# An order from 600 drawn-up plans in place of one list schedule, in a fused two-layer block with conditioning

## The chip, the cores and the metric

One core of one Trainium2 chip. The metric is device time in microseconds (us) of one execution; lower is better. One more execution was taken with the hardware profiler, and all rows below come from it.

## The reference

Two sequences of 2048 rows with 512 features each, and one vector of 512 per sequence that conditions them:

```python
emb = jnp.dot(jax.nn.silu(t), ada_w) + ada_b
shift_msa, scale_msa, gate_msa, shift_mlp, scale_mlp, gate_mlp = jnp.split(emb, 6, axis=-1)
norm = _ln(x) * (1.0 + scale_msa[:, None]) + shift_msa[:, None]
h = jax.nn.gelu(jnp.dot(norm, ssm_w1) + ssm_b1, approximate=False)
x = x + gate_msa[:, None] * (jnp.dot(h, ssm_w2) + ssm_b2)
norm2 = _ln(x) * (1.0 + scale_mlp[:, None]) + shift_mlp[:, None]
hf = jax.nn.gelu(jnp.dot(norm2, ff_w1) + ff_b1, approximate=True)
return x + gate_mlp[:, None] * (jnp.dot(hf, ff_w2) + ff_b2)
```

The weights ssm_w1 and ssm_w2 are 512x512, ff_w1 is 512x1024, ff_w2 1024x512, ada_w 512x3072; all is float32.

## The kernel before, in words

The 4096 rows are cut into eight blocks of 512. A block passes norm1, the first product (`ssm1`), the second product (`ssm2`), and norm2; after all eight, pairs of blocks (`s` = 0 to 3) pass the wide product (`ff1`) and then, block by block, the last one (`ff2`). All products are done with fewer multiplications and more additions: operands are split into quarters, seven products P1 to P7 replace eight, and in the ff stages this is done twice over. The additions on operands and results run on VectorE (DVE) and GpSimd (POOL), copies and activations on ScalarE (ACT), transfers are issued by SyncE (SP) and, a few, by ScalarE. Each float32 matmul of the program shows in the trace as two passes of TensorE (PE).

Nothing is issued while the program is described. `plan.add` records an `Op`: the engines that may do it (`"vg"` is VectorE or GpSimd), its cost and latency in ns on each, its size if it is a transfer, and its dependencies, found from the cells of the tiles that it reads and writes. `tt` (L256 in the profile) records a tensor-tensor op, `mm` (L294) a matmul, `turn` (L591) a transpose of VectorE, `stats` (L522 and L523) the mean and variance of a row, `act` (L274) and `copy` (L283) work of ScalarE, `dma` (L316) a transfer. So one line of the profile stands for many places, and the tiles' names (`bank` is PSUM, `hidden`, `ring`, `turned`, `near`, `far`, `rows`, `fw` are regions of SBUF that several stages share) tell them apart.

`Plan.order` then draws up the order. TensorE's order is that of the description and never changes. Every TensorE op is given a due time as if TensorE never waited; going backwards, every other op gets `late`, the latest time at which it may start for its successors' sake. `simulate` runs all engines forward by the recorded costs: whenever an engine is free, of the ops that could start first it takes the one with the earliest `late` (with a few rules about ops that become ready shortly, about transfers and about the SBUF port that VectorE and GpSimd share, `lock`). The whole is done twice, the second time with the due times moved by the wait found at the anchor, the first matmul of the first block's `ssm1`. The order of the starts is the order in which the ops are issued to the engines; on the chip each engine runs its own queue in this order and waits by semaphores.

The diff touches `Plan` alone; all stages call it through `plan.add`, and it is called at the end:

```python
for op in plan.order():
    op.done = op.fn(plan.engines[op.on])
    if op.after:
        tc.add_manual_dep(op.done.ins, op.after.done.ins.name, behind, reason="port")
```

Of the kernel before, what the change touches and what calls it, by code (L numbers as in the profile page):

```python
# [1 line left out]

# [12 lines left out]


class Op:
    __slots__ = ("n", "engs", "fn", "cost", "lat", "shared", "size", "lead", "care", "after", "done", "sooner", "deps", "succ", "late", "on", "start", "end", "note")


class Plan:
# [11 lines left out]
    LITTLE = 1 << 15  # L33
    LANES = 8
    AHEAD, SLACK = 2500.0, 150.0

    def __init__(self, nc):
        self.nc = nc
        self.engines = {"p": nc.tensor, "v": nc.vector, "a": nc.scalar, "g": nc.gpsimd, "s": nc.sync}
        self.ops, self.wrote, self.read, self.known = [], {}, {}, {}  # L40
        self.stage, self.care = "", 0.0
# [44 lines left out]
        return op  # L86

    def order(self):
        ops = self.ops
        for op in ops:  # L90
            if op.engs == "p":
                op.deps = {d for d in op.deps if ops[d].engs != "p"}
            for d in op.deps:
                ops[d].succ.append(op.n)
        t, due = 0.0, {}
        for op in ops:
            if op.engs == "p":
                due[op.n] = t
                t += op.cost["p"]
        for _ in range(2):  # L100
            for op in reversed(ops):
                late = due.get(op.n, 1e9)
                for s in op.succ:
                    late = min(late, ops[s].late - (1 + op.care) * (self.HOP + min(op.lat.values()) + op.size / self.RATE))
                op.late = late - op.sooner
            self.simulate()
            wait = ops[self.anchor].start - due[self.anchor]
            due = {n: t + wait for n, t in due.items()}
        return sorted(ops, key=lambda op: (op.start, op.n))

    def simulate(self):
        ops, hop = self.ops, self.HOP
# [1386 lines left out]
```

## Time and profile before

| | |
|---|---|
| median of 3 runs | 566.54 us (566.49 to 567.19) |
| the profiled execution's own time | 566.59 us |
| its span, first to last instruction | 564.8 us |
| granted TensorE clock | 1.000 |
| busy: TensorE, VectorE, GpSimd, ScalarE | 557.8, 483.1, 379.0, 266.0 us |
| DMA | 119.85 MB, mean 212 GB/s |

A timeline row reads: start, duration, engine, line, operation, tiles out<-in, partitions x elements, how many, and in brackets the engine's idle time before it and what ended it. Equal neighbours are merged into one row. A group's row gives busy time and the mean length of one record, then the idle time before its records. A row of waits gives total, count and longest. Of a matmul the end is modelled, and records of neighbours overlap.

### The profile page before, as it was taken

How to read it: one execution, taken by the hardware profiler on the slowest of the kernel's cores; microseconds unless marked ns; L12 is line 12 of the kernel's file. 1: busy time of each engine (PE TensorE's matmuls, PEld its weight loads, DVE VectorE, ACT ScalarE, POOL GpSimd, SP SyncE). 2: the span in 40 equal slices, each digit the busy share in tenths (PEclk: the TensorE clock that was granted, in tenths of full speed). 3: DMA queues.
4: the chain of work that ended last, by engine and by line, in shares of the span. 5: the costliest groups of instructions: out<-in, count | busy, mean ns of one | idle time of the engine just before them, and what ended most of it. 6: DMA issues, size and time to landing. Idle time of an engine off the chain costs nothing.

```text
span 564.8 us, 10322 instructions
## 1 busy us (share of the span) xinstructions
PE 557.8 (99%) x3553; PEld 506.3 (90%) x3553; DVE 483.1 (86%) x918; ACT 266.0 (47%) x534; POOL 379.0 (67%) x514
## 2 busy tenths in 40 slices
PE   8999999999999999999999999999999999999997
PEld 4888889888898988889999889999889999888997
DVE  5696978888879989898989899999999888789776
ACT  3473856674888845557102347212366122336120
POOL 2887638979826687995547866776776784446660
PEclk9999999999999999999999999999999999999999
DMA  8953799989799879895047899078956041820022
GB/s 315 398 221 87 233 343 308 316 240 320 223 268 369 257 271 273 273 323 185 4 147 255 302 286 332 18 204 282 321 172 198 2 151 46 272 95 28 1 75 74
DMA packets 53057, 119.85 MB, mean 212 GB/s; under 512 B 5473, under 2 KB 10509, under 8 KB 51470
## 3 DMA queue, kind: packets, MB, share of 16 engines
q1 hardware_dynamic: 51842, 118.66, 63.9%
q8 instruction: 28, 0.46, 0.3%
q10 hardware_dynamic: 1164, 0.55, 0.3%
q14 instruction: 23, 0.19, 0.1%
HBM read 77.63 MB, written 40.51 MB: 209 GB/s over the span
## 4 chain that ended last, share of the span: by engine, by line
PE 94%; DVE 3%; DMA 1%; issue 1%; POOL 0%; SPq 0%; DVEq 0%
PE bank L294 94%; DMA fw<-in_L_cond_ada_w_dram 1%; DVE hidden L256 1%; DVE near L256 0%; DVE marks L522 0%; PE bank L304 0%; POOL hidden L256 0%; POOL near L256 0%; SPq L316 0%; DVE rows L256 0%; DVE ring L256 0%; DVE fw L256 0%; DVE far L591 0%; DVE turned L656 0%; DVE marks L523 0%
## 5 line engine op out<-in xcount | busy, mean ns | idle before, releaser
L294 PE MATMUL bank<-turned,ring 128*128 128x256 f32 x896 | 208.7, 380 | 0.2 <-DVE turned L656 0.2
L294 PEld LDWEIGHTS bank<-turned,ring 128*128 128x128 f32 x896 | 167.6, 190 | 22.9 <-DVE turned L656 0.5
L256 DVE TENSOR_TENSOR hidden<-bank,hidden 128x512 f32<-128x512 f32 (+1 forms) x171 | 125.2, 755 | 28.0 <-PE bank L294 24.8
L294 PE MATMUL bank<-near,hidden 128*128 128x256 f32 (+1 forms) x470 | 95.3, 350 | 0.3 <-DVE rows L256 0.2
L294 PEld LDWEIGHTS bank<-near,hidden 128*128 128x128 f32 x470 | 82.1, 190 | 10.0 <-DVE rows L256 0.6
L294 PE MATMUL bank<-fw,hidden 128*128 128x128 f32 x640 | 90.4, 275 | 0.0
L256 DVE TENSOR_TENSOR rows<-bank,rows 128x128 f32<-128x128 f32 (+3 forms) x154 | 78.8, 554 | 11.4 <-PE bank L294 10.9
L294 PE MATMUL bank<-ring 128*128 128x256 f32 x336 | 82.4, 381 | 0.5 <-DVE hidden L256 0.5
L294 PEld LDWEIGHTS bank<-fw,hidden 128*128 128x128 f32 x640 | 81.2, 192 | 0.4
L283 ACT COPY bank<-bank 128x512 f32<-128x512 f32 (+2 forms) x88 | 37.3, 425 | 83.3 <-PE bank L294 82.2
L256 POOL TENSOR_TENSOR turned<-turned 128x512 f32<-128x512 f32 (+1 forms) x56 | 63.1, 1139 | 16.7 <-ACT turned L274 9.4
L294 PEld LDWEIGHTS bank<-ring 128*128 128x128 f32 x336 | 63.2, 190 | 11.2 <-issue 1.7
L294 PE MATMUL bank<-fw,far 128*128 128x128 f32 (+2 forms) x644 | 67.6, 278 | 0.7 <-DMA fw<-in_L_cond_ada_w_dram 0.7
L294 PEld LDWEIGHTS bank<-fw,far 128*128 128x128 f32 (+1 forms) x644 | 60.9, 167 | 2.7 <-issue 1.7
L274 ACT ACTIVATE hidden<-hidden,cols 128x512 f32<-128x512 f32 (+1 forms) x66 | 45.0, 712 | 37.9 <-DVE hidden L256 37.8
L294 PE MATMUL bank<-fw,near 128*128 128x128 f32 (+1 forms) x452 | 61.1, 279 | 0.0
L256 POOL TENSOR_TENSOR hidden<-hidden 128x128 f32<-128x128 f32 (+2 forms) x52 | 43.6, 847 | 22.6 <-DVE hidden L256 6.4
L294 PEld LDWEIGHTS bank<-fw,near 128*128 128x128 f32 x452 | 56.0, 192 | 0.4
L256 POOL TENSOR_TENSOR fw<-fw 128x256 f32<-128x256 f32 (+1 forms) x52 | 45.0, 875 | 13.3 <-DVE fw L256 7.7
L274 ACT ACTIVATE turned<-turned,mod,mod 128x512 f32<-128x512 f32 x56 | 41.5, 805 | 8.2 <-DMA turned<-turned 7.2
L256 POOL TENSOR_TENSOR ring<-turned,ring 128x256 f32<-128x256 f32 x37 | 27.8, 757 | 15.8 <-PE bank L294 9.7
L256 DVE TENSOR_TENSOR hidden<-hidden 128x512 f32<-128x512 f32 (+2 forms) x58 | 34.9, 621 | 1.2 <-ACT hidden L274 0.8
(136 smaller groups left out, 692.4 us busy)
## 6 DMA issues: line engine op xcount, KB each, us to landing
ring<-fw_parts SPq DMA_DIRECT2D x28, 512.0 KB
turned<-far SPq DMA_DIRECT2D x52, 256.0 KB
ring<-fw_parts SPq DMA_DIRECT2D x28, 384.0 KB
rows<-x SPq DMA_DIRECT2D x32, 256.0 KB
turned<-turned SPq DMA_DIRECT2D x32, 256.0 KB
out_dram<-rows SPq DMA_DIRECT2D x28, 256.0 KB
fw_parts<-fw SPq DMA_DIRECT2D x21, 256.0 KB
fw<-in_L_cond_ada_w_dram SPq DMA_DIRECT2D x5, 1024.0 KB
```

Of the source, the lines that this page charges most:

```text
L256: lambda E: E.tensor_tensor(o, a, b, f),
L274: lambda E: E.activation(o, a, func, bias=bias, scale=scale),
L283: plan.add("a", lambda E: E.copy(o, a), [o], [a], {"a": cost}, {"a": cost + 60})
L294: lambda E: E.matmul(o, lhsT, rhs, start=start, stop=stop, skip_group_check=True, **kw),
```

## The change

`order` first draws up the same plan as before (`draw_up` with an empty `wanted`, twice, with the same shift of the due times in between). Then it makes 600 rounds. In each it changes `wanted`, a table of ops that are to be placed some time sooner (their `late` is lowered): it picks one wait of TensorE behind the anchor, longer waits more often, goes from the inputs that were late there back by up to eight steps along the latest inputs, and wants the op found there sooner by a multiple of the wait; in 3 of 10 rounds it also drops one older wish. The plan is drawn up anew by the unchanged `simulate`, and `follow` then runs its sequence, with the order on every engine fixed, in three cases: transfers that land 700 ns after their data has passed, 2200 ns, and 1200 ns at 85% of the rate. The cost of a plan is the mean of TensorE's end over the three. A worse plan may be kept on the way, by up to 300 ns at first and less and less later; the best one found is issued. The random numbers have a fixed seed. The ops, their costs, their dependencies and TensorE's order are the same; `simulate` is not changed.

```diff
+    ROUNDS, WARMTH, LEAST = 600, 300.0, 30.0
+    CASES = ((700.0, 1.0), (2200.0, 1.0), (1200.0, 0.85))
...
     def order(self):
...
-        t, due = 0.0, {}
-        for op in ops:
-            if op.engs == "p":
-                due[op.n] = t
-                t += op.cost["p"]
-        for _ in range(2):
-            for op in reversed(ops):
-                late = due.get(op.n, 1e9)
-                for s in op.succ:
-                    late = min(late, ops[s].late - (1 + op.care) * (self.HOP + min(op.lat.values()) + op.size / self.RATE))
-                op.late = late - op.sooner
-            self.simulate()
-            wait = ops[self.anchor].start - due[self.anchor]
-            due = {n: t + wait for n, t in due.items()}
-        return sorted(ops, key=lambda op: (op.start, op.n))
+        tensor = [op for op in ops if op.engs == "p"]
+        t = 0.0
+        for op in tensor:
+            op.due, t = t, t + op.cost["p"]
+        self.draw_up({})
+        wait = ops[self.anchor].start - ops[self.anchor].due
+        for op in tensor:
+            op.due += wait
+        draw = random.Random(1)
+        wanted, (cost, gaps) = {}, self.draw_up({})
+        best = cost, wanted
+        for n in range(self.ROUNDS):
+            other = dict(wanted)
+            if other and draw.random() < 0.3:
+                del other[draw.choice(list(other))]
+            for d, over in draw.choices(gaps, [g[0] for g in gaps])[0][1]:
+                for _ in range(draw.choice((0, 0, 1, 2, 3, 5, 8))):
+                    before = [u for u in ops[d].deps if ops[u].engs != "p"]
+                    if not before:
+                        break
+                    d = max(before, key=lambda u: ops[u].end)
+                other[d] = other.get(d, 0.0) + over * draw.choice((0.5, 1.0, 1.5, 3.0))
+            found = self.draw_up(other)
+            if found[0] <= cost + draw.random() * self.WARMTH * (1 - n / self.ROUNDS):
+                wanted, (cost, gaps) = other, found
+                if cost < best[0]:
+                    best = cost, wanted
+        self.draw_up(best[1])
+        return self.sequence
+
+    def draw_up(self, wanted):
+        ops = self.ops
+        for op in reversed(ops):
+            late = op.due if op.engs == "p" else 1e9
+            for s in op.succ:
+                late = min(late, ops[s].late - (1 + op.care) * (self.HOP + min(op.lat.values()) + op.size / self.RATE))
+            op.late = late - op.sooner - wanted.get(op.n, 0.0)
+        self.simulate()
+        self.sequence = sorted(ops, key=lambda op: (op.start, op.n))
+        cost, gaps = 0.0, []
+        for landing, pace in self.CASES:
+            cost += self.follow(landing, pace, gaps) / len(self.CASES)
+        return cost, gaps
+
+    def follow(self, landing, pace, gaps):
+        ops, hop, end = self.ops, self.HOP, [0.0] * len(self.ops)
+        free = dict.fromkeys("pvags", 0.0)
+        pipe, lock, lanes = 0.0, 0.0, [0.0] * self.LANES
+        for op in self.sequence:
+            e = op.on
+            ready = 0.0
+            for d in op.deps:
+                t = end[d] if ops[d].on == e and not ops[d].size else end[d] + hop
+                if t > ready:
+                    ready = t
+            start = max(free[e], ready)
+            if op.size:
+                start = max(start, lanes[0])
+                pipe = max(start + self.FLIGHT, pipe) + op.size / (self.RATE * pace)
+                end[op.n] = (pipe if op.size > self.LITTLE else start + op.lat[e]) + landing
+                lanes = lanes[1:] + [end[op.n]]
+            else:
+                if e in op.shared:
+                    start = max(start, lock)
+                    lock = start + op.cost[e]
+                end[op.n] = start + op.lat[e]
+            if e == "p" and start > free[e] + self.LEAST and op.n > self.anchor:
+                gaps.append((start - free[e], [(d, end[d] + hop - free[e]) for d in op.deps if end[d] + hop > free[e]]))
+            free[e] = start + op.cost[e]
+        return free["p"]
```

More of the change, by code (lines that the diff above doesn't have):

```diff
@@ L1 @@
+import random
 from contextlib import ExitStack
@@ L17 @@
 class Op:
-    __slots__ = ("n", "engs", "fn", "cost", "lat", "shared", "size", "lead", "care", "after", "done", "sooner", "deps", "succ", "late", "on", "start", "end", "note")
+    __slots__ = ("n", "engs", "fn", "cost", "lat", "shared", "size", "lead", "care", "after", "done", "sooner", "deps", "succ", "due", "late", "on", "start", "end", "note")
 class Plan:
```

## The prediction

> **What bounds the kernel now.** I read the page first, then TensorE's waits, then its groups by form, then its timeline at each wait, and last the timelines of VectorE and GpSimd at the same places.
>
> ```profile
> span 564.8 us, 10322 instructions
> ...
> PE 557.8 (99%) x3553; PEld 506.3 (90%) x3553; DVE 483.1 (86%) x918; ACT 266.0 (47%) x534; POOL 379.0 (67%) x514
> ...
> PE 94%; DVE 3%; DMA 1%; issue 1%; POOL 0%; SPq 0%; DVEq 0%
> ```
>
> TensorE is busy 99% of the span and makes 94% of the chain that ended last. A new order can take away nothing of its work, only its waits. The list of its waits is short:
>
> ```profile
> PE bank L294 <- POOL small L321: 1.3, 1, 1.3
> PE bank L294 <- DMA fw<-in_L_cond_ada_w_dram: 0.7, 2, 0.4
> PE bank L294 <- DVE hidden L256: 0.5, 2, 0.2
> PE bank L294 <- DVE rows L256: 0.2, 1, 0.2
> PE bank L294 <- DVE turned L656: 0.2, 1, 0.2
> ```
>
> The columns are total, count and longest, in us. The first two rows belong to the first 11 us, before the op that the planner uses as its anchor; the rest make 0.9 us. But a matmul's record runs past the start of the next one (its end is modelled), so short waits hide in it. So I add up the work that TensorE must do, from its groups by form and from stretches without a wait:
>
> ```profile
> L294 PE MATMUL bank<-turned,ring 128*128 128x256 f32 x896 | 208.7, 380 | 0.2 <-DVE turned L656 0.2
> L294 PE MATMUL bank<-ring 128*128 128x256 f32 x336 | 82.4, 381 | 0.5 <-DVE hidden L256 0.5
> L294 PE MATMUL bank<-near,hidden 128*128 128x256 f32 x336 | 75.0, 380 | 0.3 <-DVE rows L256 0.2
> ...
> L294 PE MATMUL bank<-far 128*128 128x512 f32 x10 | 7.1, 863 | 1.3 <-POOL small L321 1.3
> L294 PE MATMUL bank<-fw,far 128*32 128x128 f32 x192 | 6.5, 276 | 0.7 <-DMA fw<-in_L_cond_ada_w_dram 0.7
> L304 PE MATMUL bank<-far 128*128 128x128 f32 x32 | 4.3, 276 | 0.0
> L294 PE MATMUL bank<-fw,near 128*128 128x256 f32 x16 | 3.6, 379 | 0.0
> L294 PE MATMUL bank<-fw,far 128*128 128x256 f32 x16 | 3.6, 379 | 0.0
> ```
> ```profile
> 14.07 5.45 PE L294 MATMUL bank<-turned,ring 128*128 128x256 f32 x24 [0.21 <-DVE turned L656]
> 19.45 1.08 PE L294 MATMUL bank<-fw,far 128*32 128x128 f32 x32
> 20.46 5.45 PE L294 MATMUL bank<-turned,ring 128*128 128x256 f32 x24
> 32.04 1.04 PE L304 MATMUL bank<-far 128*128 128x128 f32 x8
> 33.12 3.07 PE L294 MATMUL bank<-near,hidden 128*128 128x256 f32 x13
> 204.75 3.19 PE L294 MATMUL bank<-near,hidden 128*128 128x256 f32 x14
> 208.17 4.15 PE L294 MATMUL bank<-near,hidden 128*128 128x256 f32 x18 [0.24 <-DVE rows L256]
> 253.23 1.89 PE L294 MATMUL bank<-turned,ring 128*128 128x256 f32 x8
> 255.36 1.10 PE L294 MATMUL bank<-ring 128*128 128x256 f32 x4 [0.24 <-DVE hidden L256]
> 342.68 1.10 PE L294 MATMUL bank<-ring 128*128 128x256 f32 x4 [0.24 <-DVE hidden L256]
> 426.56 2.77 PE L294 MATMUL bank<-turned,ring 128*128 128x256 f32 x12
> 429.34 1.10 PE L294 MATMUL bank<-ring 128*128 128x256 f32 x4
> 560.26 0.61 PE L294 MATMUL bank<-fw,hidden 128*128 128x128 f32 x4
> ```
> ```profile
> 515.91 44.97 PE bank L294 x396
> ```
>
> One pass with 256 columns: the 14 from 204.75 take 3.19 us, and one record is 0.38 us long, so (3.19 - 0.38)/13 = 0.216 us from start to start; the overhang of a record is 0.38 - 0.22 = 0.16 us. One pass with 128 columns: the last row of the chain holds four passes of 256 and 392 of 128, (44.97 - 0.16 - 4 x 0.216)/392 = 0.112 us. The five rows of 128x256 hold 896 + 336 + 336 + 16 + 16 = 1600 passes; of 3553 records, less these, the 10, the 192, the 32 and one small one, 1718 passes of 128 are left. From the first matmul of the first block (14.07 us) on that makes 1600 x 0.216 = 345.6, 1718 x 0.112 = 192.4, about 4 groups of 32 narrow passes at 20.46 - 19.45 = 1.01 each = 4.0, and some 16 transposes at about 0.11 = 1.8: 543.8 us. What passed is 560.26 + 0.61 - 0.16 - 14.07 = 546.6 us. So **all that any order can win behind 14 us is about 2.8 us**, 0.5% of the run; half a nanosecond in the 0.216 is 0.8 us of that, so 2 to 3.6.
>
> **The change part by part.** Instructions, bytes and TensorE's own order stay; what can move is the order on VectorE, ScalarE, GpSimd and the two DMA issuers, and which of VectorE and GpSimd takes an op that both may do. With nothing wanted the new code draws up the old order first, so it starts from the trace above and keeps another one only if TensorE ends earlier in the mean of its three cases. The question is how much of the 2.8 us sits where a queue's order made it.
>
> The waits, by the rows above. Before 208.17: the 14 passes from 204.75 are issued through by 204.75 + 14 x 0.216 = 207.77, 0.40 us lost. Before 255.36: 253.23 + 8 x 0.216 = 254.96, 0.40 lost; before 342.68 the same idle 0.24 us shows, so 0.40 again. Before 429.34: 426.56 + 12 x 0.216 = 429.15, 0.19 lost, which the record covers; I take the same at the end of the fourth of these stages, 515.91. Before 33.12: eight transposes at about 0.11 from 32.04 end at 32.92, 0.20 lost. The group behind a wait also runs longer: four passes at 0.216 and the overhang would be 1.02, and the rows show 1.10, so 0.08 us more for each. Six places: 0.40 x 3 + 0.19 x 2 + 0.20 + 6 x 0.08 = 2.3 us. The other 0.5 is spread in bits that I don't place.
>
> Now what the queues held there:
>
> ```profile
> 204.52 0.69 DVE L256 TENSOR_TENSOR ring<-bank,ring 128x512 f32<-128x512 f32 x1 [0.19 <-PE bank L294]
> ...
> 206.86 0.68 DVE L591 STREAM_TRANSPOSE far<-near 128x512 f32<-128x512 f32 x1
> 207.46 0.65 DVE L256 TENSOR_TENSOR rows<-bank,rows 128x512 f32<-128x512 f32 x1
> ```
> ```profile
> 250.84 4.37 DVE L256 TENSOR_TENSOR hidden<-bank,hidden 128x1024 f32<-128x1024 f32 x5 [0.50 <-PE bank L294]
> ```
> ```profile
> 425.24 4.55 DVE L256 TENSOR_TENSOR hidden<-bank,hidden 128x1024 f32<-128x1024 f32 x5
> 429.71 1.02 DVE L256 TENSOR_TENSOR hidden<-hidden 128x512 f32<-128x512 f32 x1
> ```
> ```profile
> 30.54 1.29 POOL L256 TENSOR_TENSOR hidden<-hidden 128x512 f32<-128x512 f32 x1
> 31.77 2.53 POOL L256 TENSOR_TENSOR near<-near 128x512 f32<-128x512 f32 x2
> ```
> At 207.46 the add that TensorE waits for stands behind a transpose of the next norm (0.68 us). Before the transpose it would end 0.6 us sooner, and the whole 0.48 goes; the transpose then comes 0.65 us later, ahead of ScalarE's and a DMA's work for a stage that starts tens of us later, so I cost that at nothing (0.65 us on VectorE's queue if that cover were gone). At 250.84 VectorE had stood idle 0.50 us for TensorE and then does five adds without a pause; another add in that idle time moves the last one up by at most 0.5 us, but it also waits for its own matmul, so I take 0.35 of the 0.48, here and in the next such stage. At 425.24 there is no idle time left in the run of adds, and I take nothing for the two small waits of 429.34 and 515.91. At 33.12 the sum in near stands behind a sum in hidden of 1.29 us on GpSimd; the other way round TensorE's 0.28 goes. In all 0.48 + 2 x 0.35 + 0.28 = 1.5 us within reach; from 0, if none is hit, to the 2.8 that the work leaves. I take two thirds, 1.0, since 600 drawn changes in an order of some 2,000 ops off TensorE (the counts in the page's first part) hit some and not all, and leave 0.1 for new waits of a few tens of ns: **0.9 us**.
>
> The cost that is compared ends with TensorE. What lies behind (560.87 to 564.8, 3.9 us, and 1.8 more up to the execution's own 566.59) isn't in it; its work is a last add and a store, fixed by data, 0 +- 0.2. The head, up to 14.07, waits for the first weights (the 0.7 above) and isn't drawn on by the gaps, which count behind the anchor only: 0 here, +-0.5, since a step back along the inputs may reach a first load.
>
> The second and third case assume transfers that land 1.5 and 0.5 us later, the third also at 85% of the rate. TensorE has no wait for a DMA in the list but the 0.7 us at the head, so what is won in these two cases alone is worth nothing on the chip, and may be paid for with the first. The Trainium skill (DMA: Bandwidth & Descriptors, Latency and other measured facts) gives the access to HBM as 0.2 us on average and 2 us at high load, which would make the late cases the true ones; this trace has no wait of TensorE for a transfer in its loaded middle, so the sum doesn't use it.
>
> **The rivals.** *More of it goes*: the adds at 429 and 515 and the unplaced half microsecond too, 1.8 of 2.8 us: 564.8. For it: the waits are few, short and repeated by stage, so one shift serves several; VectorE is 86% busy, so it has room. Against: 425.24 without idle time.
>
> *The late cases win*: the search mends waits that only its late transfers have and leaves those of the trace: 566.5. For it: two of three cases are late. Against: the waits of the trace stand in all three cases.
>
> *VectorE's queue turns against it*: work for late loads is pulled forward and stands ahead of the adds that release TensorE's banks, as at 206.86. Its price is the row of that place: one op of 0.68 us in a wrong place costs 0.48 us. There are four stages like the one at 250.84 with a run of adds as long as TensorE's own work; two such ops in each make 8 x 0.48 = 3.8 us, less 0.9 won: 569.5; with one in each and one in half of the second products, 6 x 0.48 - 0.9 = +2.0: 568.6, which I take. It decides above 0.9/0.48, two such places. Against: the plan's own gaps are what is compared.
>
> *The shared port*: an op that moves to GpSimd beside VectorE. At 429.71 VectorE's hidden<-hidden took 1.02 us; the same size from a bank took 0.65 at 207.46, so 0.37 us more. The six places would give 6 x 0.37 = 2.2, less 0.9: 567.9. The Trainium skill (SBUF — State Buffer, SBUF: two separate sides) says that VectorE with two inputs in SBUF and GpSimd share a port pair by an exclusive lock, held for the whole instruction; the 1.02 agrees with a part of such a block. The new code counts a lock for such ops in its cases, so I give it little.
>
> **How the numbers follow.** Forecast (0.38): 566.59 - 0.9 = 565.7, which stands the same to the median of 566.54. More of it 0.30, late cases 0.11, queue 0.16, port 0.05. About 0.2% (1.1 us) is what a measurement of this kernel can tell from no change. Faster by more than that: 0.27 of the 0.30, and a quarter of the forecast's 0.38 (its gain is 0.3 to 1.5), 0.37. Slower: 0.15 of the queue's, 0.04 of the port's and 0.01 of the rest, 0.20. The same: 0.43. The range: the forecast's own is 565.1 to 566.3; down to 564.2 it leaves out a quarter of "more of it", and up to 568.4 half of the queue's: 0.07 and 0.09 outside.
>
> **What would show it.** Right: behind 14 us the idle rows "<-DVE rows" near 208 and "<-DVE hidden" near 255 and 343 are gone or below 0.1 us, TensorE's first block still starts near 14.07, and the stretch from there to its end is 545.1 to 546.3 us; VectorE's adds at 207 stand ahead of the transpose. Wrong: new idle rows of TensorE behind DMA or VectorE in the stages at 75 to 255 us, a longer start, or a stretch of over 547.7 us; the same rows at the same places would mean that only the late cases were mended.

## The result, and the profile after

| | before | after |
|---|---|---|
| median | 566.53 us (22 runs) | 567.41 us (22 runs) |
| lowest to highest | 566.44 to 567.26 | 566.74 to 568.55 |
| ratio, with 95% interval | | 1.0013 (1.0007 to 1.0019) |
| span of the profiled execution | 564.8 us | 565.5 us |
| first block's first matmul starts | 14.07 us | 14.82 us |
| from there to the end of the last matmul | 546.80 us | 546.75 us |

The change is slower by 0.13%, 0.9 us; the forecast was 0.9 us faster. The last two rows, of the two profiled executions, say where: the stretch that the search was made for is as long as it was, and the 0.75 us that are lost lie ahead of it, in the head. (The line numbers of the changed kernel are 61 higher: `tt` is L317, `mm` L355, the transposes by TensorE L365, statistics L583 and L584; the experiments' helpers shift them again.)

TensorE's waits after, total, count, longest:

```profile
PE bank L355 <- POOL small L382: 1.3, 1, 1.3
PE bank L355 <- DVE hidden L317: 0.8, 2, 0.4
PE bank L365 <- DMA fw<-in_L_cond_ssm_b_dram: 0.7, 1, 0.7
PE bank L365 <- DVE far L642: 0.6, 1, 0.6
PE bank L355 <- DMA fw<-in_L_cond_ada_w_dram: 0.3, 1, 0.3
PE bank L355 <- DVE turned L717: 0.2, 1, 0.2
```

Two rows are new, both on the head's transposes (L365). The head on its timeline, after:

```profile
5.52 0.18 DVE L584 BATCH_NORM_AGGREGATE marks<-marks 128x2 f32<-128x6 f32 x1
...
7.50 0.23 PE L365 MATMUL bank<-far,fw 44*128 44x44 f32 x1 [0.72 <-DMA fw<-in_L_cond_ssm_b_dram]
...
7.77 0.20 DVE L1415 COPY cols<-bank 128x44 f32<-128x44 f32 x1 [2.07 <-PE bank L365]
7.89 1.27 DVE L583 BATCH_NORM_STATS2 marks<-far 128x6 f32<-128x512 f32 x2
...
11.76 1.25 PE L365 MATMUL bank<-far 128*128 128x128 f32 x8 [0.58 <-DVE far L642]
```

and the same place before:

```profile
6.33 0.69 DVE L522 BATCH_NORM_STATS2 marks<-far 128x6 f32<-128x512 f32 x1 [0.17 <-DMA far<-in_x_dram]
6.95 0.30 DVE L523 BATCH_NORM_AGGREGATE marks<-marks 128x2 f32<-128x6 f32 x2
...
7.30 0.23 PE L304 MATMUL bank<-far,fw 44*128 44x44 f32 x1
...
7.57 0.20 DVE L1354 COPY cols<-bank 128x44 f32<-128x44 f32 x1 [0.32 <-PE bank L304]
...
11.17 1.09 PE L304 MATMUL bank<-far 128*128 128x128 f32 x8
```

The copy `cols<-bank` reads what TensorE makes of the small rows (biases and the conditioning vectors). Before, VectorE did statistics of two more row groups first and reached the copy about when its input was there. The new order puts the copy right behind the first group's statistics. VectorE then stands idle for 2.07 us until the small rows have landed and TensorE has turned them, the statistics start late, and TensorE's first transposes begin at 11.76 in place of 11.17 us. The chain of the changed kernel names the transfer:

```profile
2.05 5.32 DMA fw<-in_L_cond_ssm_b_dram
```

It landed 5.3 us after its issue. The planner's `dma` gives such small loads 2.0 us, so in the plan the copy waits for little there. A second number of the plan is too small at the same place: `mm` costs a matmul with 512 columns 0.853 us, so the four that stand ahead of the small matmul take 3.4 us in the plan, while their eight passes took 5.4 us in this profile and 6.3 and 6.7 us in those of e2 and e1 below.

Behind the head no wait of TensorE for rows is listed any more; the add at 208 us stands ahead of the transpose:

```profile
207.30 0.67 DVE L317 TENSOR_TENSOR rows<-bank,rows 128x512 f32<-128x512 f32 x1
207.89 0.70 DVE L652 STREAM_TRANSPOSE far<-near 128x512 f32<-128x512 f32 x1
```

The wait near 33 us is gone as well, and those near 255 and 342 are shorter, but two others grew. TensorE at the end of the first and of the third wide product, after:

```profile
252.36 2.85 PE L355 MATMUL bank<-turned,ring 128*128 128x256 f32 x12
255.22 1.10 PE L355 MATMUL bank<-ring 128*128 128x256 f32 x4
...
426.50 2.75 PE L355 MATMUL bank<-turned,ring 128*128 128x256 f32 x12
429.67 1.10 PE L355 MATMUL bank<-ring 128*128 128x256 f32 x4 [0.42 <-DVE hidden L317]
```

Twelve passes at 0.216 us from 426.50 end at 429.09; 429.67 is 0.58 us later, where it was 0.19 before. The fourth product does the same (516.67, idle 0.42). From 252.36 to 255.22 are 2.86 us, 0.27 over the twelve passes, where 0.40 was lost before. In the second product, 339.65 to 342.61, it is 0.37 against 0.40. VectorE and GpSimd ahead of 429, after:

```profile
423.25 1.23 DVE L317 TENSOR_TENSOR hidden<-bank,hidden 128x1024 f32<-128x1024 f32 x1
424.39 0.85 DVE L317 TENSOR_TENSOR near<-hidden 128x512 f32<-128x512 f32 x1
425.17 4.36 DVE L317 TENSOR_TENSOR hidden<-bank,hidden 128x1024 f32<-128x1024 f32 x5
```
```profile
423.41 1.28 POOL L317 TENSOR_TENSOR near<-hidden 128x512 f32<-128x512 f32 x1 [0.42 <-DVE hidden L317]
...
426.62 1.28 POOL L317 TENSOR_TENSOR hidden<-hidden 128x512 f32<-128x512 f32 x1
```

and VectorE before, just ahead of the run at 425.24 that the prediction shows:

```profile
423.31 2.02 DVE L256 TENSOR_TENSOR hidden<-bank,hidden 128x1024 f32<-128x1024 f32 x2
```

Before, the short slot behind 424.6 us held a second add in hidden, so one add less was left for the run that TensorE waits for. After, a sum in near that GpSimd had done takes that slot, for 0.85 us beside GpSimd's own op, and the add is done inside the run. GpSimd does the sum in hidden at 426.62 in exchange, which VectorE did at 429.71. In all, a net 14 ops have moved from GpSimd to VectorE (500 and 932 instructions where there were 514 and 918).

TensorE's order is the same in both kernels, so the starts of its matmuls can be compared one by one. From the first block's first matmul to the one near 375 us the kernel before takes 360.92 us and the changed kernel 360.11; from there to the end they take 185.88 and 186.65. So the search wins 0.8 us up to there and loses 0.8 behind it. No run shows a reason why the two should be equal.

### The profile page after: what moved, and what is told of

The parts are those of the page before. It is cut to its first block, busy times and chain, and to the rows that moved or that the text cites. A ratio compares the mean times of both kernels' runs of the same rounds, so it can differ in the third digit from the quotient of the medians.

```text
span 565.5 us, 10324 instructions
## 1 busy us (share of the span) xinstructions
PE 557.4 (99%) x3553; PEld 505.7 (89%) x3553; DVE 490.4 (87%) x932; ACT 263.6 (47%) x534; POOL 364.8 (65%) x500
## 4 chain that ended last, share of the span: by engine, by line
PE 93%; DVE 3%; issue 2%; DMA 1%; ACTq 0%; POOL 0%; DVEq 0%
PE bank L355 92%; DVE hidden L317 2%; DMA fw<-in_L_cond_ssm_b_dram 1%; PE bank L365 1%; DVE near L317 0%; ACTq L377 0%; DVE marks L583 0%; POOL marks L617 0%; DVE far L642 0%; DVE turned L717 0%; DVE rows L317 0%; DVE bank L542 0%; DVE cols L1415 0%; POOL marks L616 0%; DVEq L1555 0%
## 5 line engine op out<-in xcount | busy, mean ns | idle before, releaser
L355 PE MATMUL bank<-turned,ring 128*128 128x256 f32 x896 | 209.1, 380 | 0.2 <-DVE turned L717 0.2
L355 PEld LDWEIGHTS bank<-turned,ring 128*128 128x128 f32 x896 | 167.3, 190 | 23.6 <-issue 0.9
L317 DVE TENSOR_TENSOR hidden<-bank,hidden 128x512 f32<-128x512 f32 (+1 forms) x171 | 123.9, 753 | 22.5 <-PE bank L355 19.4
L355 PE MATMUL bank<-near,hidden 128*128 128x256 f32 (+1 forms) x470 | 95.0, 349 | 0.0
L355 PEld LDWEIGHTS bank<-near,hidden 128*128 128x128 f32 x470 | 82.2, 190 | 9.2
L355 PE MATMUL bank<-fw,hidden 128*128 128x128 f32 x640 | 90.3, 275 | 0.0
L317 DVE TENSOR_TENSOR rows<-bank,rows 128x128 f32<-128x128 f32 (+3 forms) x154 | 78.6, 555 | 11.1 <-PE bank L355 9.5
L355 PE MATMUL bank<-ring 128*128 128x256 f32 x336 | 82.5, 381 | 0.9 <-DVE hidden L317 0.8
L355 PEld LDWEIGHTS bank<-fw,hidden 128*128 128x128 f32 x640 | 81.3, 192 | 0.4
L355 PEld LDWEIGHTS bank<-ring 128*128 128x128 f32 x336 | 63.1, 190 | 11.7 <-POOL near L317 1.6
L317 POOL TENSOR_TENSOR turned<-turned 128x512 f32<-128x512 f32 (+1 forms) x56 | 61.6, 1112 | 10.9 <-DVE turned L317 5.6
L355 PE MATMUL bank<-fw,far 128*128 128x128 f32 (+2 forms) x644 | 67.6, 278 | 0.5 <-DMA fw<-in_L_cond_ada_w_dram 0.3
L317 POOL TENSOR_TENSOR hidden<-hidden 128x512 f32<-128x512 f32 (+2 forms) x48 | 43.3, 909 | 31.6 <-DVE hidden L317 10.2
L355 PEld LDWEIGHTS bank<-fw,far 128*128 128x128 f32 (+1 forms) x644 | 60.9, 167 | 2.4 <-issue 1.3
L355 PE MATMUL bank<-fw,near 128*128 128x128 f32 (+1 forms) x452 | 61.1, 279 | 0.0
L355 PEld LDWEIGHTS bank<-fw,near 128*128 128x128 f32 x452 | 56.0, 192 | 0.4
L317 POOL TENSOR_TENSOR fw<-fw 128x256 f32<-128x256 f32 (+1 forms) x49 | 43.6, 898 | 16.3 <-DVE fw L317 9.4
L317 POOL TENSOR_TENSOR ring<-turned,ring 128x256 f32<-128x256 f32 x37 | 27.2, 743 | 18.1 <-PE bank L355 12.6
L317 DVE TENSOR_TENSOR hidden<-hidden 128x512 f32<-128x512 f32 (+2 forms) x62 | 35.6, 588 | 1.6 <-POOL hidden L317 1.2
```

Source lines behind the costliest of these rows:

```text
L317: lambda E: E.tensor_tensor(o, a, b, f),
L355: lambda E: E.matmul(o, lhsT, rhs, start=start, stop=stop, skip_group_check=True, **kw),
```

## The experiments

Theory A: the loss of 0.75 us is made in the head by the one copy; and behind it what the search wins is given back by the one exchange at 424 us and its twin in the fourth product. Rivals: B, the loss is made behind the anchor by the new order as a whole; C, the run of adds sets the wait whatever stands ahead of it; D, VectorE and GpSimd have no room at all, so that what one wait loses another gains; and the late cases, for which the search may have given up what it won in the first. For moved ops the order is otherwise kept on each engine: a helper takes op `n` out of the sequence, puts it behind another, and lets ops that depend on it follow.

| run | median, us | ratio to before (95%) | start, us | start to TensorE's end, us |
|---|---|---|---|---|
| e1_copy_back | 566.47 | 0.9999 (0.9991 to 1.0008) | 14.01 | 546.76 |
| e2_copy_early | 566.80 | 1.0012 (1.0003 to 1.0020) | 14.96 | 546.77 |
| e3_and_adds | 578.14 | 1.0199 (1.0185 to 1.0213) | 14.01 | 559.57 |
| e4_true_landing | 566.45 | 0.9999 (0.9990 to 1.0008) | 14.00 | 546.78 |
| e5_adds_back | 567.18 | 1.0012 (1.0003 to 1.0021) | 13.99 | 547.37 |
| e6_first_case | 566.57 | 1.0002 (0.9993 to 1.0011) | 14.00 | 546.71 |
| e7_adds_late | 567.72 | 1.0022 (1.0013 to 1.0031) | 14.01 | 548.00 |
| e8_spliced | 565.76 | 0.9987 (0.9978 to 0.9996) | 14.08 | 546.07 |

The kernel before took 566.51 to 566.53 us beside them. The last two columns are of the profiled executions.

**The copy back in its place (e1).**

```diff
-        return self.sequence
+        return self.moved(self.sequence, ((38, 93),))   # op 38, the copy, behind op 93, an aggregate
```

> The changed kernel with one VectorE op moved back: in the head the copy of the small rows' columns (cols<-bank) stands again behind the first three statistics and their aggregates, as before the change; every other queue is as in the changed kernel. Theory A (the loss is made in the head: the copy waits for a small transfer, and the statistics wait behind it): the first block starts at 14.07 us again instead of 14.82, and the whole takes 567.4 - 0.75 = 566.65 us, within 0.1% of the kernel before. Rival B (the loss is made behind the anchor, by the new order of VectorE and GpSimd): the start moves or not, the time stays at 567.2 to 567.6.

566.47 us, 0.94 under the changed kernel, by one op of VectorE in another place; 11 runs lie between 566.40 and 566.62. The start:

```profile
7.98 0.26 PE L388 MATMUL bank<-far,fw 44*128 44x44 f32 x1
...
14.01 2.21 PE L378 MATMUL bank<-turned,ring 128*128 128x256 f32 x9 [0.21 <-DVE turned L740]
```

The small matmul came even later than in the changed kernel (7.98 against 7.50 us), and the first block still starts at 14.01: behind the statistics the copy may wait for its input without cost. Rival B falls.

**The copy early in the kernel before (e2).**

```diff
-        return sorted(ops, key=lambda op: (op.start, op.n))
+        return self.moved(sorted(ops, key=lambda op: (op.start, op.n)), ((38, 27),))   # behind the first aggregate
```

> The kernel before with that one copy moved ahead, directly behind the first statistics and their aggregate, as the change has it; nothing else is changed. Theory A: the start of the first block goes from 14.07 to about 14.8 us and the whole to 566.5 + 0.75 = 567.3 us. Rival B: 566.5 us as before. If something of each holds, between.

The profiled execution shows the whole effect, VectorE idle at the copy and the start at 14.96 us:

```profile
7.91 0.20 DVE L1377 COPY cols<-bank 128x44 f32<-128x44 f32 x1 [2.29 <-PE bank L327]
```

The times fall in two groups: six at 566.59 to 566.80 and five at 567.43 to 567.96. The effect was thus 0.1 to 0.3 us in some executions and 0.9 to 1.4 in the others, 0.12% in the comparison; the expected 567.3 lies between the groups, and the median in the lower one. What the copy waited for isn't the same in the two profiles either. In the changed kernel's it was the landing. In this one the chain that ended last runs through TensorE's eight passes with 512 columns, and no transfer stands in it:

```profile
1.35 6.33 PE bank L317 x8
```

In e2 these passes start 0.85 to 1.0 us apart up to the seventh, and 0.47 us lie between the last two; in the changed kernel 0.43 us lie between them from the fifth on. Either time, of the landing or of the passes, may differ from one execution to the next, and would then explain the two groups and the wide range of the changed kernel; only the profiled executions show them, so this stays argued.

**The model's number for the small loads (e4).**

```diff
-            dma(rows_t[r0:r1, :], src, "a")
+            dma(rows_t[r0:r1, :], src, "a", lat=5300.0)
```

> The changed kernel with one number of its model altered: the four small loads of the head are planned to land 5.3 us after their issue, as the trace shows, instead of 2.0; the search of 600 plans runs anew from there. Theory A: the new plan keeps the statistics ahead of the copy, starts the first block at about 14.1 us, and, with other orders behind it that are as good in the plan as the changed kernel's, takes 566.3 to 566.9 us. Rival B: a plan of this search loses behind the anchor as well, 567.2 us or more with a start at 14.1.

566.45 us: with 5.3 us in its model the search keeps the copy behind three statistics with their aggregates, and TensorE starts the first block at 14.00 us. (5.3 us also covers the passes that the plan counts too short.) e6 below, a second search with this number, starts at 14.00 too. That the 2.0 us made the first search move the copy is argued from these two; no run shows which wish moved it. Behind the start it wins nothing either (546.78 us), with other waits than the changed kernel's: near 429 the 0.42 us idle again, not so near 516.

**The exchange at 424 and 511 us, undone with a fault (e3).**

```diff
+        return self.moved(self.sequence, ((38, 93), (3119, 3116), (3167, 3138), (3702, 3699), (3750, 3721)))
         # 3119 and 3702: the adds in hidden; 3167 and 3750: the sums near<-hidden, here behind the run
```

> As e1_copy_back, and in the wide products of pairs 2 and 3 the add of a result in hidden goes back into VectorE's idle slot, ahead of the sum in near<-hidden that the change had moved from GpSimd to VectorE; that sum goes behind the run of adds. Theory A with its second part (the two waits of 0.58 us near 429 and 516 come from that one op in VectorE's idle slot): both waits fall to about 0.17 us, so 566.65 - 2 x 0.41 = 565.8 us, 0.13% under the kernel before. Rival C (the run of adds is as long as TensorE's work whatever stands ahead of it): the waits stay, 566.65 us.

578.14 us; this is a miss of the experiment. The kernel carries an ordering wait (`op.after`) from some GpSimd ops to the VectorE op whose port use precedes them in the plan. The sum that I moved back was one of these, and GpSimd stood behind it:

```profile
422.58 1.27 POOL L340 TENSOR_TENSOR near<-hidden 128x512 f32<-128x512 f32 x1 [0.42 <-DVE hidden L340]
429.04 1.26 POOL L340 TENSOR_TENSOR near<-near,hidden 128x512 f32<-128x512 f32 x1 [5.18 <-DVE near L340]
```

It says nothing on theory A or C, but it shows how an op moved on one queue holds another.

**The exchange undone with the sums on GpSimd again (e5).**

```diff
+        for n, behind, next in ((3167, 3157, 3158), (3750, 3740, 3741)):
+            ops[n].on, ops[n].after, ops[next].after = "g", None, None
+        return self.moved(self.sequence, ((38, 93), (3167, 3157), (3119, 3116), (3750, 3740), (3702, 3699)))
```

> As e1_copy_back, and in the wide products of pairs 2 and 3 the sum near<-hidden goes back to GpSimd behind the sum before it, as in the kernel before, with its port wait dropped, and the add in hidden takes VectorE's idle slot again. (e3_and_adds had left that sum on VectorE but later; GpSimd's next op carries an ordering wait for it, and its queue stood 5 us behind it.) Theory A, second part: TensorE's waits of 0.58 us near 428 and 515 fall to about 0.17, so 566.47 - 2 x 0.41 = 565.65 us, 0.15% under the kernel before. Rival C (the run of adds sets the wait whatever stands ahead): 566.45 us.

The time is a miss, and the waits are as expected: near 428 and 515 TensorE now loses 0.17 us each, so C falls. But the stretch grew by 0.6 us over e1, so 0.6 + 2 x 0.41 = 1.4 us come back later, in places that had hardly a wait there; the largest:

```profile
449.86 0.61 PE L380 MATMUL bank<-fw,hidden 128*128 128x128 f32 x4
450.72 0.71 PE L380 MATMUL bank<-fw,hidden 128*128 128x128 f32 x4 [0.25 <-DVE rows L342]
```

Four passes at 0.112 from 449.86 end at 450.31, 0.41 us lost. The rest of the changed kernel's order there was drawn up with these sums on VectorE and the sums in hidden on GpSimd. GpSimd now has both, one more op of 1.27 us, and VectorE comes to wait for it:

```profile
428.85 1.53 DVE L342 TENSOR_TENSOR near<-near 128x512 f32<-128x512 f32 x2 [0.54 <-POOL near L342]
```

That all of the 1.4 us come from this op fits, but isn't shown step by step.

**The exchange made in the kernel before (e7).**

```diff
+        for n in (3167, 3750):
+            ops[n].on, ops[n].after = "v", None
+        return self.moved(sorted(ops, key=...), ((3167, 3116), (3119, 3125), (3750, 3699), (3702, 3708)))
```

> The kernel before with only the change's arrangement at two places, the wide products of pairs 2 and 3: the sum near<-hidden moves from GpSimd to VectorE, into the slot ahead of the run of adds, and one add in hidden moves from that slot into the run. Theory A, second part: TensorE's waits near 429 and 516 grow from 0.17 to about 0.58 us, 566.5 + 2 x 0.41 = 567.3 us. Rival C: 566.5 us as before.

567.72 us, 1.2 slower and 0.4 more than expected. The wait before the last four passes is the changed kernel's, and another stands within the twelve ahead of it:

```profile
426.48 2.96 PE L319 MATMUL bank<-turned,ring 128*128 128x256 f32 x12
429.87 1.10 PE L319 MATMUL bank<-ring 128*128 128x256 f32 x4 [0.42 <-DVE hidden L281]
```

From 426.48 to 429.87 are 3.39 us, 0.80 over the twelve passes, against 0.19 before: 0.61 more at each of the two places, 1.2 in all. So the exchange alone costs all that this run loses, and more here than the 0.4 us for each place in the changed kernel. The moved sum took longer:

```profile
424.37 1.10 DVE L281 TENSOR_TENSOR near<-hidden 128x512 f32<-128x512 f32 x1
```
```profile
423.65 1.27 POOL L281 TENSOR_TENSOR near<-hidden 128x512 f32<-128x512 f32 x1 [0.67 <-ACT hidden L299]
```

It had to wait longer for GpSimd's op beside it (see the shared port below): 1.10 us in place of 0.85, which is about the difference.

**Without the late cases (e6).**

```diff
-    CASES = ((700.0, 1.0), (2200.0, 1.0), (1200.0, 0.85))
+    CASES = ((700.0, 1.0),)
```
(with the true landing of e4)

> As e4_true_landing (small loads of the head planned at 5.3 us), and the plans are compared in the first case alone, transfers that land 700 ns after their data; the two cases with late transfers are left out. If the late cases cost what the search wins in the first (the rival of late cases), this should end lower than e4_true_landing, by 0.3 us or more, near 566.1 us. If the search ends in the same kind of order with either cost, the waits behind 14 us stay at about 3 us in all, with 0.58 us near 428 or 515 again, and the time at 566.4 to 566.6 us.

566.57 us and 546.71 us behind the start, with both waits of 0.42 idle again. A search without the late cases comes to the same two waits, so they are not what costs.

**The two orders joined (e8).**

```diff
-        self.draw_up(best[1])
-        return self.sequence
+        self.draw_up({})
+        old = [(op, op.on, op.after) for op in self.sequence]
+        self.draw_up(best[1])
+        new = [(op, op.on, op.after) for op in self.sequence]
+        return self.spliced(new, old, 2803)   # new up to this matmul of ff2, old from there; op 38 behind op 93
```

> The two orders joined: the changed kernel's order on every engine up to a matmul at 375 us (with the head's copy moved back as in e1_copy_back), and from there the order of the kernel before, with its ops on its engines. Theory A with its second part (the search wins about 0.9 us ahead of this place, and loses as much in the last two wide products): the first block starts near 14.0 us, the rows before 208 and 33 are gone, the waits near 254 and 341 are 0.17 us and those near 428 and 515 are 0.17 us too; 566.47 - 2 x 0.41 = 565.65 us, 0.15% under the kernel before. Rival D (VectorE and GpSimd have no room: what is taken from one wait comes back in another whichever order is chosen, as in e5_adds_back): 566.4 us or more.

Ordering waits that no longer lead from GpSimd to VectorE are left out. 565.76 us, 0.13% under the kernel before and 0.3% under the changed one. TensorE's waits no longer name VectorE behind the start, but for its first matmul:

```profile
PE bank L393 <- POOL small L420: 1.3, 1, 1.3
PE bank L393 <- DMA fw<-in_L_cond_ada_w_dram: 0.4, 2, 0.2
PE bank L393 <- ACT bank L382: 0.2, 1, 0.2
PE bank L393 <- DVE turned L755: 0.2, 1, 0.2
```
```profile
425.55 2.77 PE L393 MATMUL bank<-turned,ring 128*128 128x256 f32 x12
428.32 1.10 PE L393 MATMUL bank<-ring 128*128 128x256 f32 x4
```

The stretch is 546.07 us, 0.7 under both kernels. So rival D falls too: there is room, and the search's order up to 375 us holds it (360.11 us up to there, as in the changed kernel, and 185.96 behind it, 0.1 more than in the kernel before). The run takes back the whole order behind 375 us and not the exchange alone; that the exchange makes the loss there rests on its two waits in the changed kernel and on e7.

## Why the prediction was wrong

**That only waits can be won, at most about 2.8 us,** was not contradicted: the changed kernel and all runs but e3 lie between 546.1 and 548.0 us behind the start, and the lowest of them wins 0.7.

**The step that failed first is the head**, costed as "0 here, +-0.5". The reason given was that the gaps that are drawn lie behind the anchor. The step named the way in, a step back along the inputs may reach an op of the head, but priced it by the transfers to be loaded and not by VectorE's queue. It cost 0.75 us in the profile (14.07 to 14.82). What I would have needed stood in the trace of before: the small loads are issued by 2.4 us, and the small matmul that reads them stands at 7.30 us, so whatever depends on it must not come ahead of the statistics. e1 takes this one move back and with it 0.94 us; e2 makes it alone, and its profiled execution starts 0.89 us later than the kernel before.

**The forecast's 0.9 us behind the head** failed in two of its terms. Held: the waits near 33 and 208, which were read as the fault of one op ahead in a queue, are gone, and by the starts of the matmuls 0.31 and 0.50 us came where 0.28 and 0.48 were taken. Mis-sized: at 255 and 342 I took 0.35 each, and 0.13 and 0.03 came; there too the search has put a sum that GpSimd did before into VectorE's run of adds. And the largest: the two waits for which I took "nothing", with "0.1 for new waits" in all, grew from 0.19 to 0.58 us each, 0.8 together. The stretch moved by 0.05 us. The argument for "nothing" was that VectorE has no idle time in its run of adds; that told me that nothing could be won there, and I did not turn it round: where there is hardly any slack, one more op costs more than half of its length. (The merged row at 425.24 hides two pauses of 0.13 and 0.09 us ahead of the add that TensorE waits for.) The add of 0.69 us cost 0.39 us for each place in the changed kernel; e7 is the exchange alone, 0.6 us for each place; and e8, which leaves it out with the rest of the new order behind 375 us, has a stretch 0.7 us shorter than either kernel's.

**The rival of VectorE's queue** had this mechanism, with a price of 0.48 us for one op in a wrong place (0.39 was measured in the changed kernel, 0.6 in e7) and its threshold of two places (0.9/0.48): two places were hit, and the balance was near zero, as it says. Its picture of work pulled forward for late loads was not what happened: e6, without the late cases, has the same two waits.

**The shared port.** This rival, priced at 0.37 us for each op and given little, is seen in the trace, in the other direction: the ops moved from GpSimd to VectorE. Alone, a sum of this size with both inputs in SBUF takes VectorE 0.68 us:

```profile
428.21 0.68 DVE L340 TENSOR_TENSOR near<-hidden 128x512 f32<-128x512 f32 x1
```

That is e3, with GpSimd idle. Started while an op of GpSimd was under way, such sums took longer:

| VectorE's sum | took, us | GpSimd's op had still to go | longer than 0.68 by |
|---|---|---|---|
| before, 429.71 | 1.02 | 0.47 | 0.34 |
| changed kernel, 424.39 | 0.85 | 0.30 | 0.17 |
| e7, 424.37 | 1.10 | 0.55 | 0.42 |
| changed kernel, 253.07 | 1.32 | 0.78 | 0.64 |
| changed kernel, 340.44 | 1.15 | 0.61 | 0.47 |

The delay is each time what GpSimd's op still had to go, less 0.13 to 0.14 us. This agrees with the rule of the Trainium skill (SBUF — State Buffer, SBUF: two separate sides), by which the one that starts first holds the shared ports for its whole instruction and the other is blocked. At 424.39 the delay is a part of the exchange's price. At 253.07 it is 0.64 us right ahead of the add that TensorE waits for at 255.22:

```profile
253.07 1.32 DVE L317 TENSOR_TENSOR near<-near,hidden 128x512 f32<-128x512 f32 x1
```
```profile
251.34 2.51 POOL L317 TENSOR_TENSOR near<-hidden 128x512 f32<-128x512 f32 x2
```

That may be why only 0.13 of the 0.35 us came there; no run has this sum at another time.

**The landing of transfers.** I weighed the figures of the Trainium skill for the access to HBM (DMA: Bandwidth & Descriptors, Latency and other measured facts) by TensorE's waits in the loaded middle and found none. That holds after the change too. The place where a landing decided was the head, at 5.3 us for rows of a few KB issued beside the loads of x and the first weights.

What stays open: why the early copy costs the changed kernel less in some executions than in others (566.74 to 568.55), and why the search, with the landing put right (e4), still ends no lower than the kernel before. That its plans count the wait near 429 as smaller than the chip's 0.58 us would explain the latter; no run tested that.

## What to carry to other kernels

When an order is drawn up by a model, look for the ops whose time in the model is furthest from the trace, and put those numbers right before searching: here an op placed by a latency of 2.0 us for 5.3, and by first matmuls of 3.4 us for 5.4 and more, cost 0.9 us, about as much as the search won ahead of 375 us. A search that aims at waits in one part still moves ops in the others, so compare start, middle and end as stretches of their own. Where an engine's run has hardly any idle time ahead of a wait, price both what can be taken out and what one more op would add.

## What was not expected of the hardware

A transfer of a few KB issued at 2.05 us on ScalarE's queue landed after 5.3 us while loads of x and of the weights were under way. TensorE's first eight passes with 512 columns took 5.4 us in one profile and 6.7 in another (changed kernel, e1).

With one op waiting for either early in VectorE's queue, executions of the same program spread over 1.4 and 1.8 us (566.59 to 567.96 in e2, 566.74 to 568.55 in the changed kernel). With the op behind other work they spread over 0.2 us in e1, but over 0.8 in the kernel before and 1.3 in e8, so the spread isn't this op's alone.

A sum of VectorE with both inputs in SBUF waited for an op of GpSimd that was under way, and took up to 1.32 us in place of 0.68.
